# Reordering the prologue of an adaLN block, and one expert's loads on another queue

## The chip, the cores and the metric

The kernel runs on one core of a Trainium2 chip. The metric is the device time of one execution in microseconds (us). Engines: TensorE (PE; its weight loads are PEld), VectorE (DVE), ScalarE (ACT), GpSimd (POOL) and SyncE (SP), which here only issues DMAs. ScalarE can issue DMAs too. Each engine runs its own instructions in order, and waits for the others by semaphores.

## The reference

A transformer block with adaptive LayerNorm on x of 8 batch elements x 512 rows x 256 columns, all in fp32:

```python
mod = (silu(c) @ wmod).reshape(8, 6, 1, 256)
sa, ca, ga, sb, cb, gb = (mod[:, i] for i in range(6))
ga, gb = (sign of each) * maximum(abs of each, 0.25)
h = layernorm(x) * (1 + ca) + sa
x = x + ga * attention(h)          # gated delta rule
h = layernorm(x) * (1 + cb) + sb
x = x + gb * experts(h)            # 2 of 6 experts per batch element
```

The attention projects h to q and k (16 heads of 128), v and z (32 heads), runs a causal convolution of 4 taps and a SiLU over q, k and v, and then a gated delta rule in chunks, whose decays come from h as well:

```python
beta = sigmoid(h @ W_b);  g = -exp(A_log) * softplus(h @ W_a + dt_bias)
g = cumsum(g within a chunk);  decay = exp(g[i] - g[j]) for j <= i
```

The experts take the mean of h over the 512 rows, choose the two best of six, and compute `gelu(h @ W1 + b1) @ W2 + b2` for both, weighted by a softmax of the two.

## The kernel before, in words

The work is cut into 128 pairs: 8 batch elements x 16 key heads, each with its two value heads. A chunk is 128 rows, so a batch element has 4. The steps of a pair (`wk`, `pk`, `ck`, ... with places in the table `PLACE`, L26) are spread over about 13 turns of 1000 places each, so that many pairs are in flight; L1292 sorts all steps of all pairs by turn and place, and they are issued in that order under a manual schedule. The side steps of a batch element are put among them: `after_attention(b)` (L325: second LayerNorm, experts) and `before_attention(b + 1)` (L232: first LayerNorm of the next element, its beta and its decays).

What stands ahead of the manual schedule is arranged by the framework's own scheduler: the constants, the block `pro` (L478 to L524) and `before_attention(0)` (L525). In `pro`, ScalarE's queue loads the modulation's weights `wm` (ten of the twelve column blocks) and `wg6` (the two gates), SyncE's the condition `ct` and small tensors. `mps` (L501) is the modulation for both LayerNorms: 8 blocks x 2 halves of the contraction = 16 matmuls of 8 columns, which the profile shows as 32 records. `gps` (L512) is the gates; four DVE instructions (L518 to L521) make them at least 0.25 in size, and L522 writes them to DRAM (`gates_far`), from where `gates(b)` (L172) spreads them much later.

`before_attention(0)` begins with `norm_transposed` (L178): statistics on DVE, `rs` by a power on POOL (L195), then xn = (x - mean) * rs on DVE (L200, eight pieces, four buffers), transposes on TensorE (`lnT`, L208) and scale and shift on ScalarE (`ha`, L216). Then `ba` (L241: 8 matmuls), `beta` (L249), the softplus as a series (L253 to L284: 18 DVE instructions and one exp on ScalarE), the sums of the decays (`dec`, L292), their exp (`ex`, L297), `G` and `neg` (L301, L303), `G` transposed (`Gt`, L308, L312) and written to DRAM (`gfar`, L316).

For each pair, SyncE loads `wk` (L570, two DMAs of 128 KB) and `gb` (L585: rows of `gfar`, spread to 128 partitions, 512 KB). TensorE projects `prk` and `prq` (L614), ScalarE makes tap 0 (L626), DVE taps 1 to 3 (L630), ScalarE the SiLU (`kqa`, L643). Transposes `kt` and `qt` follow, their squares on ScalarE (`jk` L676, `jq` L712), roots on POOL (`kept`, L682), and the decays of the pair: `dca` (L724) reads `gb` and `G` on ScalarE, exp (L732). A change of function set on ScalarE shows as ACT_TABLE_LOAD.

`wk` lives in the pool `wp` (L538), which takes the memory of the pool `pro` after it has been released, so its first load waits for the last users of `pro`. PSUM has six banks for turns (`bank`, L112).

In the last batch element `after_attention(7)` has nothing beside it. `expert(k)` (L381) and `expert_biases(k)` (L395) each load the chosen index into a register of the issuing engine (L379), and then issue three DMAs for the weights and four for the biases, all on SyncE. `gelu` (L427) needs the biases; its second third holds hidden units of both experts.

Of the kernel before, what the change touches and what calls it, by code (L numbers as in the profile page):

```python
# [15 lines left out]
P = 128  # L16
# [71 lines left out]
def adaln_block(  # L88
# [26 lines left out]
    def bank(name):  # L115
        return banks.tile([P, 512], F32, name=name, tag="b")
# [208 lines left out]
    def after_attention(b):  # L325
# [50 lines left out]
            f["v2"] = tiny("b2", [P, 2, DM])  # L376

        def of_choice(k):
            return nc.sync.value_load(f["ix"][0:1, k : k + 1], min_val=0, max_val=NE - 1)  # L379

        def expert(k):  # L381
            if k == 0:
                experts()
            e = of_choice(k)
            nc.sync.dma_start(
                f["s1"][:, :, k * DFF : (k + 1) * DFF],
                w1[bass.ds(e, 1)].rearrange("e (kt p) f -> p (e kt) f", p=P),
            )
            for at, t, q, n in hidden_parts(k, 0, DFF):
                nc.sync.dma_start(  # L390
                    f["s2"][q : q + n, t, :],
                    w2[bass.ds(e, 1), at : at + n, :].rearrange("e p m -> (e p) m"),
                )

        def expert_biases(k):  # L395
            e = of_choice(k)
            for half in range(2):
                for at, t, q, n in hidden_parts(k, half * FP, FP):
                    at -= half * FP
                    nc.sync.dma_start(  # L400
                        f["v1"][q : q + n, t : t + 1],
                        b1[bass.ds(e, 1), at : at + n, half : half + 1].rearrange("e p t -> p (e t)"),
                    )
            nc.sync.dma_start(f["v2"][:, k, :], b2[bass.ds(e, 1)].to_broadcast([P, DM]))

        def weigh():

# [67 lines left out]
        return steps  # L475


    with tc.tile_pool(name="pro", bufs=1) as pro:  # L478
        ct = pro.tile([P, NKT, NB], F32, name="ct")
        nc.sync.dma_start(ct, cond.rearrange("(kt p) b -> p kt b", p=P))  # L480
        wm = pro.tile([P, NKT, 10, P], F32, name="wm")
        nc.scalar.dma_start(
            wm, wmod[:, : 10 * P].rearrange("(kt p) (i m) -> p kt i m", p=P, m=P)
        )
        wg6 = pro.tile([P, 2, NKT, DM], F32, name="wg6")
        for i, col in enumerate((2 * DM, 5 * DM)):
            nc.scalar.dma_start(
                wg6[:, i], wmod[:, col : col + DM].rearrange("(kt p) m -> p kt m", p=P)
            )
        nc.sync.dma_start(wba, w_ba.rearrange("(kt p) m -> p kt m", p=P))  # L490
        nc.sync.dma_start(dtb, dt_bias.partition_broadcast(P))
        nc.sync.dma_start(alog, a_log.partition_broadcast(P))
        nc.sync.dma_start(cw, conv_w)
        nc.sync.dma_start(nw, norm_w)
        nc.sync.dma_start(gwt, gate_w.rearrange("(kt p) e -> p kt e", p=P))
        nc.scalar.activation(silu_c, ct, AF.Silu)

        mps = bank("mps")
        for i, col in enumerate((0, 1, 2, 3, 6, 7, 8, 9)):
            for kt in range(NKT):  # L500
                mm(  # L501
                    mps[:, i * NB : (i + 1) * NB], wm[:, kt, col, :], silu_c[:, kt, :],
                    start=kt == 0, stop=kt == NKT - 1,
                )
        nc.vector.tensor_copy(modt, mps[:, : 8 * NB].rearrange("p (i b) -> p i b", b=NB))
        for i in (2, 6):
            nc.vector.tensor_scalar_add(modt[:, i : i + 2, :], modt[:, i : i + 2, :], 1.0)

        gps = bank("gps")
        for i in range(2):  # L510
            for kt in range(NKT):
                mm(  # L512
                    gps[:NB, i * DM : (i + 1) * DM], silu_c[:, kt, :], wg6[:, i, kt, :],
                    start=kt == 0, stop=kt == NKT - 1,
                )
        gv, ga = (pro.tile([NB, 2 * DM], F32, name=n) for n in ("gv", "ga"))
        nc.scalar.copy(gv, gps[:NB])
        nc.vector.scalar_tensor_tensor(ga, gv, -1.0, gv, ALU.mult, ALU.max)  # L518
        nc.vector.tensor_scalar_max(ga, ga, 0.25)
# [17 lines left out]
    with ExitStack() as st:  # L537
# [800 lines left out]
```

## Time and profile before

| | us |
|---|---|
| time, median of 3 runs (lowest, highest) | 4062.34 (4062.27, 4062.44) |
| time of the profiled execution | 4061.08 |
| its span, first to last instruction | 4059.4 |
| PE busy, share of the span | 3847.1, 95% |
| DVE busy | 3528.6, 87% |
| ACT busy | 3169.1, 78% |
| POOL busy | 1462.0, 36% |

Lines of the profile: an `L` number is the line of the kernel; `out<-in` are tiles by their names in the program with buffer numbers left out; `xN` counts instructions. A timeline line is start, duration, engine, line, operation, and in brackets the idle time ahead of it with the one who ended it. SPq and ACTq are the queues' own instructions, such as the issue of a DMA. A chain line is start, duration and what it was. A line for a stretch of time gives for PE, PEld, DVE, ACT and POOL busy time (and instructions), then the granted TensorE clock, the DMA engines' busy share, and GB/s.

### The profile page before, as it was taken

Reading aid. Unit: us, or ns where it says so; the run is one execution under the profiler, and the core shown is the slowest. Engines: PE = TensorE matmul, PEld = TensorE weight load, DVE = VectorE, ACT = ScalarE, POOL = GpSimd, SP = SyncE. Lnnn points to the kernel's source line nnn. Section 1 sums busy time; section 2 is a strip of 40 time slices with the busy share of each in tenths; the row PEclk is TensorE's granted clock in tenths of the full one; section 3 lists DMA queues with packets and bytes.
Section 4 is the critical chain, followed back from the end, with each engine's and each line's share of the span. In section 5 each row is a group of like instructions: output and inputs, shape, how many; then the busy total and the mean of one; then the engine's idle time right before and its main releaser. Section 6 shows DMA issues by size and latency. Waiting matters only on the chain.

```text
span 4059.4 us, 79959 instructions
## 1 busy us (share of the span) xinstructions
PE 3847.1 (95%) x24592; PEld 2771.3 (68%) x24592; DVE 3528.6 (87%) x7973; ACT 3169.1 (78%) x9809; POOL 1462.0 (36%) x1320
## 2 busy tenths in 40 slices
PE   5489999999999999999999999999999999999998
PEld 3256776767776677767777667767677667776776
DVE  4689888998989988998889988899888998899864
ACT  5578778878878788778888778888888878877664
POOL 3433333333333333433334333334333333333211
PEclk8799999999999999999999999999999999999999
DMA  4576667667666676666677566566766667666541
GB/s 119 148 182 170 184 177 192 172 173 187 158 180 185 177 179 179 169 173 185 174 177 187 161 188 178 171 184 174 184 169 172 182 179 188 164 176 179 144 115 55
DMA packets 1101589, 689.09 MB, mean 170 GB/s; under 512 B 667368, under 2 KB 964712, under 8 KB 1101168
## 3 DMA queue, kind: packets, MB, share of 16 engines
q1 hardware_dynamic: 1100352, 682.14, 63.7%
q8 instruction: 203, 3.33, 0.3%
q14 instruction: 218, 1.79, 0.1%
q10 hardware_dynamic: 816, 1.84, 0.1%
HBM read 435.68 MB, written 248.00 MB: 168 GB/s over the span
## 4 chain that ended last, share of the span: by engine, by line
PE 66%; DVE 22%; ACT 4%; issue 4%; DMA 2%; POOL 1%; SPq 0%; POOLq 0%; DVEq 0%; ACTq 0%
PE prz L1200 9%; PE prv L614 8%; PE acc L1244 7%; PE in L1153 4%; PE u L1109 4%; PE dst L1131 4%; PE kk L739 4%; PE prq L614 4%; PE pk L1079 3%; PE prk L614 3%; DVE prl L863 3%; PE pq L1084 3%; PE ot L1226 2%; DVE cvk L630 2%; PE vt L1035 2%
## 5 line engine op out<-in xcount | busy, mean ns | idle before, releaser
L1216 POOL TENSOR_TENSOR msq<-msq,mhalf 128x8 f32<-128x8 f32 x128 | 209.4, 1636 | 1228.5 <-DVE msq L1210 1228.5
L630 DVE SCALAR_TENSOR_TENSOR cvv<-prv,cw,cvv 128x511 f32<-128x511 f32 (+2 forms) x768 | 567.6, 739 | 12.3 <-ACT cvv L626 8.7
L762 POOL TENSOR_TENSOR mta<-mta,dca 128x512 f32<-128x512 f32 x256 | 366.6, 1432 | 510.7 <-DVE mta L750 297.2
L614 PE MATMUL prv<-ha,wv 128*128 128x512 f32 x1024 | 486.7, 598 | 4.5 <-DVE vr L1042 4.5
L1200 PE MATMUL prz<-ha,wz 128*128 128x512 f32 x1024 | 485.8, 597 | 1.5 <-ACT tmp L1100 0.7
L1244 PE MATMUL acc<-wo,z 128*128 128x256 f32 x2048 | 484.3, 379 | 0.5 <-DVE z L1232 0.5
L682 POOL TENSOR_TENSOR kept<-kept,half 128x8 f32<-128x8 f32 x128 | 210.1, 1641 | 727.6 <-ACT jq L712 627.7
L1244 PEld LDWEIGHTS acc<-wo,z 128*128 128x128 f32 x2048 | 378.5, 190 | 46.8 <-DVE z L1232 1.1
L769 POOL TENSOR_TENSOR dca<-qkm,dca 128x256 f32<-128x256 f32 x512 | 394.9, 792 | 32.0 <-issue 7.4
L1100 ACT ACTIVATE tmp<-pq,ex 128x128 f32<-128x128 f32 x768 | 243.5, 378 | 152.9 <-PE pq L1084 152.6
L1153 PE MATMUL in<-w,s 128*128 128x128 f32 x2048 | 317.0, 277 | 23.7 <-DVE cvk L630 19.5
L1153 PEld LDWEIGHTS in<-w,s 128*128 128x128 f32 x2048 | 298.4, 191 | 54.2 <-DVE cvk L630 25.8
L724 ACT ACTIVATE dca<-gb,G 128x128 f32<-128x128 f32 x1024 | 332.9, 428 | 2.7 <-DMA sfar<-dca 2.5
L1124 ACT ACTIVATE w<-u,kept 128x128 f32<-128x128 f32 x1024 | 302.0, 363 | 28.6 <-DVE wd L1116 27.8
L1175 ACT ACTIVATE jo<-o 128x128 f32<-128x128 f32 x1024 | 305.6, 304 | 4.1 <-DVE o L1166 0.8
L614 PEld LDWEIGHTS prv<-ha,wv 128*128 128x128 f32 x1024 | 191.8, 191 | 152.1 <-issue 124.7
L630 DVE SCALAR_TENSOR_TENSOR cvk<-prk,cw,cvk 128x511 f32<-128x511 f32 (+2 forms) x384 | 283.8, 739 | 4.3 <-ACT cvk L626 3.9
L630 DVE SCALAR_TENSOR_TENSOR cvq<-prq,cw,cvq 128x511 f32<-128x511 f32 (+2 forms) x384 | 283.4, 738 | 0.8
L1232 DVE SCALAR_TENSOR_TENSOR z<-ot,nw,z 128x512 f32<-128x512 f32 x256 | 190.8, 746 | 103.1 <-PE ot L1226 97.1
L1200 PEld LDWEIGHTS prz<-ha,wz 128*128 128x128 f32 x1024 | 180.3, 190 | 140.0 <-issue 122.9
L739 PE MATMUL kk<-kqa 128*128 128x256 f32 x1024 | 273.2, 393 | 0.0
L1090 DVE SCALAR_TENSOR_TENSOR r<-pk,neg,vr 128x128 f32<-128x128 f32 x768 | 231.6, 343 | 45.9 <-PE pk L1079 45.7
(204 smaller groups left out, 10052.1 us busy)
## 6 DMA issues: line engine op xcount, KB each, us to landing
gb<-gfar SPq DMA_DIRECT2D x128, 512.0 KB
qfar<-kqa SPq DMA_DIRECT2D x128, 512.0 KB
sfar<-dca SPq DMA_DIRECT2D x256, 256.0 KB
s<-sfar SPq DMA_DIRECT2D x256, 256.0 KB
wk<-in_dram SPq DMA_DIRECT2D x256, 128.0 KB
kfar<-kra SPq DMA_DIRECT2D x128, 256.0 KB
wv<-in_dram SPq DMA_DIRECT2D x128, 256.0 KB
kq<-qfar SPq DMA_DIRECT2D x128, 256.0 KB
```

The costliest lines, as they stand in the source:

```text
L614: mm(ps, d[wname][:, kt, j * P : (j + 1) * P], hT[:, kt, :], start=kt == 0, stop=kt == NKT - 1,)
L630: nc.vector.scalar_tensor_tensor(a[:, s:], ps[:, : SEQ - s], cw[:, ch, 3 - s : 4 - s], a[:, s:], ALU.mult, ALU.add)
L724: nc.scalar.activation(dc[:, c, h, :], d["gb"][:, 2 * gr + c, h * P : (h + 1) * P], AF.Relu, bias=rows[b]["G"][:, 2 * gr + c, k : k + 1], ...
L739: mm(ps[:, c2 * 2 * P : (c2 + 1) * 2 * P], d["kqa"][:, c, 0, :], d["kqa"][:, c].rearrange("p k i -> p (k i)"), start=True, stop=True,)
L762: nc.gpsimd.tensor_tensor(mt, mt, d["dc", gr].rearrange("p c h i -> p (c h) i"), ALU.mult)
L769: nc.gpsimd.tensor_tensor(dc, bc_mid(d["qkm", gr][:, c, :], 2), dc, ALU.mult)
L1100: nc.scalar.activation(tmp[:, h, :], d["pq", c][:, h * P : (h + 1) * P], AF.Copy, scale=rows[b]["ex"][:, 0, c, 2 * p + h : 2 * p + h + 1],)
L1124: nc.scalar.activation(w[:, h, :], d["u", c][:, h * P : (h + 1) * P], AF.Copy, scale=d["br2"][:, c, h : h + 1],)
L1153: mm(ps[:, h * P : (h + 1) * P], d["s", c, h], d["w", c][:, h, :], start=True, stop=True,)
L1175: nc.scalar.activation(junk, d["o", c // 2][:, c % 2, h, :], AF.Square, accum_out=d["msq"][:, c, h : h + 1],)
L1200: mm(ps, d["wz"][:, kt, h * P : (h + 1) * P], rows[n // HK]["ha"][:, kt, :], start=kt == 0, stop=kt == NKT - 1,)
L1244: mm(ps[:, k * DM : (k + 1) * DM], d["z", h][:, c * P : (c + 1) * P], d["wo"][:, h, :], start=p == 0 and k == 0 and h == 0, stop=p == HK - ...
```

## The change

`before_attention(0)` is no longer run as one block after `pro`. `wm` is loaded in two DMAs (4 and 6 blocks), and the modulation is computed in two halves: the first LayerNorm's, then the steps of `before_attention(0)` up to the softplus, with beta's sigmoid as the last, then the second LayerNorm's half. The gates' result `ga` gets a tile of its own outside `pro` (`gate_rows`), and its DMA to DRAM is put at the place TURN of the manual schedule. The exp of `alog` is moved up. The rest of element 0's decays (`gs`, `gx`, `gr`, `gt`, `gc`, `gl`) is put into the manual schedule just ahead of the first pair's `gb`, and so behind `wk`, `pk`, `ck`, `pq`, `cq` and `sk` of the first pair. For the last batch element's second expert (k == 1), the index load and all seven DMAs go to ScalarE's queue.

```diff
         def of_choice(k):
-            return nc.sync.value_load(f["ix"][0:1, k : k + 1], min_val=0, max_val=NE - 1)
+
+            queue = nc.scalar if b == NB - 1 and k == 1 else nc.sync
+            return queue, queue.value_load(f["ix"][0:1, k : k + 1], min_val=0, max_val=NE - 1)
...
-            e = of_choice(k)
-            nc.sync.dma_start(
+            queue, e = of_choice(k)
+            queue.dma_start(
                 f["s1"][:, :, k * DFF : (k + 1) * DFF],
...
+    first_steps = before_attention(0)
+    gate_rows = row.tile([P, 2, DM], F32, name="gate_rows", tag="of", bufs=1)
     with tc.tile_pool(name="pro", bufs=1) as pro:
...
-        nc.scalar.dma_start(
-            wm, wmod[:, : 10 * P].rearrange("(kt p) (i m) -> p kt i m", p=P, m=P)
-        )
+        for a, e in ((0, 4), (4, 10)):
+            nc.scalar.dma_start(
+                wm[:, :, a:e, :],
+                wmod[:, a * P : e * P].rearrange("(kt p) (i m) -> p kt i m", p=P, m=P),
+            )
...
-        mps = bank("mps")
-        for i, col in enumerate((0, 1, 2, 3, 6, 7, 8, 9)):
...
+        nc.scalar.activation(alog, alog, AF.Exp)
+        nc.vector.tensor_scalar_mul(alog, alog, -1.0)
+
+        def modulation(half):
+
+            ps = bank(f"mps_{half}")
+            for i in range(4):
+                for kt in range(NKT):
+                    mm(
+                        ps[:, i * NB : (i + 1) * NB], wm[:, kt, 6 * half + i, :], silu_c[:, kt, :],
+                        start=kt == 0, stop=kt == NKT - 1,
+                    )
+            m = modt[:, 4 * half : 4 * half + 4, :]
+            nc.vector.tensor_copy(m, ps[:, : 4 * NB].rearrange("p (i b) -> p i b", b=NB))
+            nc.vector.tensor_scalar_add(m[:, 2:4, :], m[:, 2:4, :], 1.0)
+
+        modulation(0)
+        for name in list(first_steps):
+            if name not in ("bsig", "gs", "gx", "gr", "gt", "gc", "gl"):
+                first_steps.pop(name)()
+        first_steps.pop("bsig")()
+        modulation(1)
...
-        gv, ga = (pro.tile([NB, 2 * DM], F32, name=n) for n in ("gv", "ga"))
+        gv = pro.tile([NB, 2 * DM], F32, name="gv")
+        ga = gate_rows[:NB].rearrange("p a b -> p (a b)")
         nc.scalar.copy(gv, gps[:NB])
...
-        nc.sync.dma_start(gates_far, ga)
-        nc.scalar.activation(alog, alog, AF.Exp)
-        nc.vector.tensor_scalar_mul(alog, alog, -1.0)
-    for step in before_attention(0).values():
-        step()
...
             order += [(at + PLACE[name], fn) for name, fn in side.items()]
+
+        order += [(PLACE["gb"] - 0.5, fn) for fn in first_steps.values()]
+        order.append((TURN, lambda: nc.sync.dma_start(gates_far, ga)))
         order.sort(key=lambda e: e[0])
```

`expert_biases` gets the same replacement of `nc.sync` by `queue` as `expert`.

More of the change, by code (lines that the diff above doesn't have):

```diff
@@ L389, in expert @@
             for at, t, q, n in hidden_parts(k, 0, DFF):
-                nc.sync.dma_start(
+                queue.dma_start(
                     f["s2"][q : q + n, t, :],
@@ L395, in expert_biases @@
         def expert_biases(k):
-            e = of_choice(k)
+            queue, e = of_choice(k)
             for half in range(2):
@@ L399, in expert_biases @@
                     at -= half * FP
-                    nc.sync.dma_start(
+                    queue.dma_start(
                         f["v1"][q : q + n, t : t + 1],
@@ L403, in expert_biases @@
                     )
-            nc.sync.dma_start(f["v2"][:, k, :], b2[bass.ds(e, 1)].to_broadcast([P, DM]))
+            queue.dma_start(f["v2"][:, k, :], b2[bass.ds(e, 1)].to_broadcast([P, DM]))
         def weigh():
@@ L496, in adaln_block @@
         nc.scalar.activation(silu_c, ct, AF.Silu)
-        mps = bank("mps")
-        for i, col in enumerate((0, 1, 2, 3, 6, 7, 8, 9)):
[L500 to L507, printed above, removed]
+        nc.scalar.activation(alog, alog, AF.Exp)
[17 more added lines that the diff above has]
+        modulation(1)
         gps = bank("gps")
```

## The prediction

> **What bounds the kernel now.** I read the page first: busy time, the slices, the chain that ended last.
>
> ```profile
> PE 3847.1 (95%) x24592; PEld 2771.3 (68%) x24592; DVE 3528.6 (87%) x7973; ACT 3169.1 (78%) x9809; POOL 1462.0 (36%) x1320
> ...
> PE   5489999999999999999999999999999999999998
> ```
>
> TensorE is full from the fourth slice (about 300 us) to the end, and it takes its work in a fixed order. So whatever is gained or lost before that, in the run-up, moves the whole stream. The change touches the first 60 us and the last 25 us only; on every engine the rest keeps its order. Next I read the timeline of the first 62 us (start, us, engine, line, operation, tiles).
>
> ```profile
> 16.63 3.63 POOL L555 MEMSET y<- 128x1024 f32 x4
> 18.62 1.72 DVE L200 TENSOR_SCALAR xn_a<-xt,mv_a,rs_a 128x128 f32<-128x128 f32 x1
> 20.69 0.33 DVE L200 TENSOR_SCALAR xn_a<-xt,mv_a,rs_a 128x128 f32<-128x128 f32 x1
> ...
> 27.02 0.90 SPq L570 DMA_DIRECT2D wk<-in_dram  x2
> ...
> 38.60 0.49 ACT L297 ACTIVATE ex<-dec 128x384 f32<-128x384 f32 x1 [7.23 <-PE dec L292]
> ...
> 39.74 3.62 PE L614 MATMUL prk<-ha,wk 128*128 128x512 f32 x4
> ...
> 40.30 0.34 SPq L316 DMA_DIRECT2D gfar<-Gt  x1
> ...
> 41.87 0.37 SPq L585 DMA_DIRECT2D gb<-gfar  x1
> ...
> 48.98 0.63 ACT L643 ACTIVATE kqa<-cvq 128x512 f32<-128x512 f32 x1 [0.50 <-DVE cvq L630]
> ...
> 50.20 1.27 ACT L724 ACTIVATE dca<-gb,G 128x128 f32<-128x128 f32 x4
> ...
> 53.58 1.64 POOL L682 TENSOR_TENSOR kept<-kept,half 128x8 f32<-128x8 f32 x1 [33.32 <-ACT jq L712]
> ```
>
> To be seen: gfar leaves at 40.30, gb is fetched at 41.87, and the first dca, which reads gb, runs at 50.20. Behind dca on ScalarE stand jq, kra, jk, jq, and the last jq releases POOL's kept at 53.58. From there the chain of waits goes kept, scalars, mta, taps of pair 1, kqa of pair 1 and so on: the last jq of the next pairs ends at about 67.4, 81.8 and 95.9, one pair each 14 us, with ScalarE almost without a gap. A delay of the first dca is therefore carried into the whole run-up. How long gb takes is in the DMA rates (last column GB/s):
>
> ```profile
> 43.00:44.00 1.00, 1.00 (x2) 0.34 (x1) 0.00 (x0) 0.56 (x1) 0.00 (x0) 1.00 0.31 89
> 47.00:48.00 1.00, 0.00 (x0) 0.00 (x0) 0.96 (x2) 0.99 (x2) 0.00 (x0) 1.00 0.88 87
> 48.00:49.00 1.00, 0.47 (x2) 0.47 (x3) 0.85 (x2) 0.50 (x2) 0.00 (x0) 0.56 0.82 186
> ```
>
> gb's 512 KB flow at 88 GB/s from 43.0, so they end at 48.5 to 48.9; with 0.3 us to the semaphore (gfar's bytes end at 41.6, gb is issued at 41.87) gb lands 7.1 us after its issue, near 49.0. The dca at 50.20 has only 1.2 us to spare. Last, the chain at the end:
>
> ```profile
> 4035.18 0.35 SPq L379
> ...
> 4043.49 2.02 DMA b<-in_dram
> 4045.51 0.02 issue
> ...
> 4045.61 0.48 ACT hid L430
> 4046.09 0.04 issue
> 4046.14 2.52 PE f L439 x10
> ```
>
> From 4035.18 to 4043.49 SyncE issues one expert DMA after another; the bias of expert 1 ends the wait of the GELU.
>
> **The change part by part: the head.** All times on the clock of the trace before.
>
> *Modulation split.* It takes 8 of 16 matmuls (3.5 of 7.0 us) from before the LayerNorm. wm's bytes stay the same, and ct, which releases silu_c at 11.40, comes behind xt on SyncE's queue as before. So the first half ends at 15.05 instead of 18.48. In the new order DVE's copy of it stands ahead of the first xn, which is ready at 15.2. POOL's memsets (L555) run until 20.26. Row: the xn of 18.62 took 1.72 us where others take 0.33; it began in the third y memset, was passed by the fourth, and ended 0.08 after it. Rule: the Trainium skill (SBUF – State Buffer, "Who interferes with whom") says that DVE's two-port modes and GpSimd share a port pair that is locked for one whole instruction, first come first served. By the rule xn would enter when the running memset ends, at about 15.7; by the row it waits for the last one, to 20.3. I take the row, as it shows a boundary (19.36) not used; the rule's sum stands with the rivals. Then: four xn to 21.1 (0.28 each), transposes 0.5 behind them, ha0 at 21.7 (before 23.04), ha1 at 23.5 (25.35): a gain of 1.8.
>
> *What is put in front of ba on PE.* The second modulation half (16 records x 0.22 = 3.5) and half of gps (4 x 0.45 = 1.8) now precede the 14 remaining ba records (3.3): 23.3+3.5+1.8+3.3 = 31.9 for g, before 29.78. Loss against before: 2.1.
>
> *Decay series and gates.* beta now stands behind g on ScalarE, with the table switch after it: sps at 34.2 (before 31.40, +2.8). The four gate rows (0.60+0.35+0.34+0.67 = 2.0) are now woven into DVE's series after the reciprocal: the last ends at 38.3.
>
> *First weights.* In the built order wk of pair 0 waits for exactly that last gate row (it reads gv, whose memory wk's pool takes over). Before it waited for gates_far, to 27.02, with 10 us to spare; now it is issued at 38.45. Its bytes before ended near 28.65, so landing is 1.9 after issue: 40.4. prk starts at 40.4, not 39.74 (+0.65). So the decays beside the projections do not bring the projections forward; the g series (7 us) is hidden, but the load has taken its place.
>
> *Projections, then decays.* prk 3.4, cvk's taps end 47.1. prq: TensorE's records went from 0.86 to 0.43 us at 44.8, 5 us after prk began; shifted or later, prq ends 46.4 (46.0 to 47.2; before 45.81). cvq to 47.15, silu table 1.28, kqa of k to 49.06. Now come the added switches: exp table 1.30, ex 0.49, G at 50.9 (before 39.12: +11.8), Gt and its copy 1.2, gfar at 52.1 (40.30), gb at 53.65, landing 60.75. kqa of q is late too, behind DVE's second and third tap (which now stand after G and Gt) and a third table: 53.5+1.3 = 54.8, to 55.4 (before 49.6), but that is covered by gb, 5 us later. dca therefore starts at 60.75 instead of 50.20: **+10.55**. wk of pair 1 follows gb on SyncE, lands at 61.6; prk and prq end near 68, when ScalarE wants them: at most 0.3, I take 0.15. gates_far moves past 8 issues to where SyncE waited 3.3 for dca: hidden; without that cover 0.4.
>
> The price of a table switch: each row of ACT_TABLE_LOAD is 1.28 and the next ACTIVATE starts 1.30 after it. The Trainium skill (ScalarE: Activation LUTs, "What ACT_TABLE_LOAD costs") gives about 2.66 us with a drain of 1.38. One added switch is on the path to gb, so the page would make the sum 1.4 larger; no row here shows the drain (cvq ends 46.54, table 46.56), so I take the row.
>
> **The tail.** Expert 1's seven DMAs (and two loads of its index) leave SyncE's queue. A row of ScalarE's queue is near SyncE's (wm 0.48 against 0.34 to 0.40). ScalarE starts after the choice's exp, at 4035.4: 2.4 us for the weights, 2.8 for the biases, which is SyncE's cadence, plus about 0.7 because its third bias now shares a semaphore with SyncE's first and waits for its landing: 4041.4. Queued behind are the GELU table and the GELUs only: table to 4042.7 (before 4044.0). Expert 1's w1 lands 2.0 earlier, so PE's 12 hidden records (0.43 each) run from 4038.56 without a gap, to 4043.75 or, if PE's pace doubles sooner than at 4045.1, 4043.1. GELU 2 ends 4044.2, and the ten records of 4046.14 start at about 4044.2. Gain 1.3 (slow pace until 4045.8) to 2.7; I take **2.0**. If ScalarE's issues took twice their time, the table would stand at 4046 and nothing would be gained.
>
> **Sum.** 10.55 + 0.15 - 2.0 = +8.7. The profiled execution took 4061.08 (span 4059.4), so 4069.8; the median of the runs, 4062.34, lies 1.26 higher: **4071.0**. 0.2% is 8.1 us, about what a measurement of this kernel can tell from no change, so the forecast lies just past it.
>
> **The rivals.**
>
> *Not slower: DVE gets in between the memsets.* Place: the first xn, 15.2. If the lock is given per memset and DVE runs several instructions on end, ha0 comes at 17.3, ba ends at 27.4, and all behind it (gates, wk, prk, gb) is 4.5 earlier: 4066.5, within 0.2%. It decides as soon as it gives back 0.6 us. For it: the rule. Against it: the row of 1.72.
>
> *Faster, as its words say: the decays are hidden.* Even with wk there in time, prk would start at 33.7, 6.7 earlier, and gb still lands at 54, 3.8 later than dca wanted it: the total would be +1.9, 4064. So a gain above 8 us would need gb off the path, and nothing in the order does that.
>
> *The run-up absorbs it.* If a DMA or PE rather than ScalarE set the pace of pairs 1 to 8, part of the 10.7 would be lost in waits that exist already: at half, 4066. Against: waits on DMA in that stretch are some 8 us for prk in 200 us, and all their DMAs are issued behind the same chain.
>
> *Worse.* If gb and wk of pair 1 delay prk by more (slow pace throughout 3.4 us), the drain of the page applies, or the ScalarE queue gains nothing: +11 to +13, 4074.
>
> **How the numbers follow.** Forecast 0.65, its own range 4069 to 4073 (PE's pace 0.7, gb's landing 0.3, tail 0.7), six tenths of it past 4070.5; DVE between the memsets 0.15; absorbed or hidden 0.08; worse 0.12. Slower: 0.65x0.6 + 0.12 and a little of the rest, 0.52; within 0.2%: 0.43; faster 0.05, for what I have not seen. Range 4065 to 4074: it takes in the first two rivals and the near end of the last.
>
> **What would show it.** xn ending at 20.3 with POOL; g near 31.9; wk issued at 38.4 behind the last gate row; two more table loads around ex; gfar at 52, dca at 60 to 61 waiting for DMA; kept at 64 (before 53.58), and the next pairs 14 us apart. In the tail ScalarE's issues done by 4041.5 plus the shift, and the GELU no longer waiting for a bias. Wrong it would be if dca starts before 57, or if the shift of kept is not found again at 300 us.

## The result: 7.6 us slower, where 8.7 were forecast

The changed kernel takes 4069.64 us (median of 18 runs, 4067.46 to 4072.79), the kernel before, on the same chip, 4062.03 (18 runs, 4060.20 to 4064.84): ratio 1.0018, interval 1.0011 to 1.0026, or +7.6 us. The profiled execution took 4068.49 against 4061.08, its span 4066.8 against 4059.4: +7.4. So the changed kernel lies near the edge of what a measurement tells from no change, and by its interval on the slower side of no change. The sum of the forecast was +8.7 (profiled execution 4069.8), the likeliest time 4071.0. About 1.3 of the 1.4 between 4071.0 and 4069.64 lie in the sum; the step from the profiled execution to the median, taken as 1.26, came out as 1.15.

The page of the changed kernel first (busy time, the slices of TensorE, and of the costliest groups the one of dca):

```profile
PE 3844.3 (95%) x24592; PEld 2768.4 (68%) x24592; DVE 3533.1 (87%) x7974; ACT 3170.8 (78%) x9811; POOL 1462.1 (36%) x1320
...
PE   5479999999999999999999999999999999999998
...
L737 ACT ACTIVATE dca<-gb,G 128x128 f32<-128x128 f32 x1024 | 332.9, 428 | 7.6 <-DMA gb<-gfar 5.4
```

TensorE is as full as before from the fourth slice on. The last line is the finding in small: of the 7.6 us that ScalarE stands idle ahead of all 1024 dca, 5.4 are one wait for gb. It is here, in the timeline of the first 70 us (start, us, engine, line, operation):

```profile
6.32 0.90 ACTq L493 DMA_DIRECT2D wg<-in_dram  x2
6.63 0.75 DVE L187 BATCH_NORM_STATS2 st_a<-xt 128x6 f32<-128x256 f32 x2 [5.53 <-DMA xt<-in_dram]
...
12.54 5.87 DVE L200 TENSOR_SCALAR xn_a<-xt,mv_a,rs_a 128x128 f32<-128x128 f32 x1
...
14.70 3.63 POOL L568 MEMSET y<- 128x1024 f32 x4
...
35.48 0.89 SPq L583 DMA_DIRECT2D wk<-in_dram  x2
37.79 3.75 PE L627 MATMUL prk<-ha,wk 128*128 128x512 f32 x4 [6.42 <-DMA wk<-in_dram]
...
48.24 0.49 ACT L297 ACTIVATE ex<-dec 128x384 f32<-128x384 f32 x1
...
49.80 0.34 SPq L316 DMA_DIRECT2D gfar<-Gt  x1
...
51.36 0.37 SPq L598 DMA_DIRECT2D gb<-gfar  x1
...
59.14 1.28 ACT L737 ACTIVATE dca<-gb,G 128x128 f32<-128x128 f32 x4 [5.41 <-DMA gb<-gfar]
...
62.52 1.64 POOL L695 TENSOR_TENSOR kept<-kept,half 128x8 f32<-128x8 f32 x1 [44.18 <-ACT jq L725]
```

ex comes at 48.24 where it was at 38.60, gfar at 49.80 (40.30), gb at 51.36 (41.87), dca at 59.14 (50.20) and kept at 62.52 (53.58). The last two are both 8.94 late. At the end of the program, where the expert numbers are found, the shift is 8.83 (4043.72 against 4034.89), and the last VectorE instruction is 7.41 late: so the tail gave back 1.42. Its chain that ended last:

```profile
4046.01 3.20 DMA w<-in_dram
4049.23 0.33 ACTq L402
...
4050.45 1.96 DMA b<-in_dram
4052.41 0.03 ACTq L432
...
4052.68 0.48 ACT hid L432
```

In this chain the GELUs stand behind a bias again, now one that ScalarE issued. The timeline shows one thing more in front of them, the load of the GELU table:

```profile
4051.38 1.28 ACT L432 ACT_TABLE_LOAD   x1 [7.15 <-DMA b<-in_dram]
```

The bias has landed at 4052.41, the table load ends at 4052.66 and the first GELU starts at 4052.68: the table load ends last, by 0.25. It stands in ScalarE's order behind ScalarE's own four bias issues, and the first of these, of 4049.23, had waited 3.20 us for the landing of SyncE's second w2 piece, because both use one completion counter (the semaphore that tells of a transfer's landing; an issue that takes it over waits until the transfer that had it before has landed).

### The profile page after: what moved, and what is told of

The parts are those of the page before. It is cut to its first block, busy times and chain, and to the rows that moved or that the text cites. A ratio compares the mean times of both kernels' runs of the same rounds, so it can differ in the third digit from the quotient of the medians.

```text
span 4066.8 us, 79963 instructions
## 1 busy us (share of the span) xinstructions
PE 3844.3 (95%) x24592; PEld 2768.4 (68%) x24592; DVE 3533.1 (87%) x7974; ACT 3170.8 (78%) x9811; POOL 1462.1 (36%) x1320
## 4 chain that ended last, share of the span: by engine, by line
PE 67%; DVE 22%; ACT 3%; issue 3%; DMA 2%; POOL 1%; SPq 0%; POOLq 0%; ACTq 0%; DVEq 0%
PE prz L1213 9%; PE prv L627 8%; PE acc L1257 7%; PE in L1166 4%; PE u L1122 4%; PE dst L1144 4%; PE prq L627 4%; PE kk L752 4%; PE pk L1092 3%; PE prk L627 3%; PE pq L1097 3%; DVE prl L876 3%; PE ot L1239 2%; PE vt L1048 2%; DVE cvk L643 2%
## 5 line engine op out<-in xcount | busy, mean ns | idle before, releaser
L1166 PEld LDWEIGHTS in<-w,s 128*128 128x128 f32 x2048 | 298.4, 191 | 52.1 <-DVE cvk L643 23.4
```

The lines of the kernel that those rows point to most:

```text
L1166: mm(ps[:, h * P : (h + 1) * P], d["s", c, h], d["w", c][:, h, :], start=True, stop=True,)
```

## Experiments

The theory on trial: the six decay steps stand behind the first projections, so gb is asked for late, and the delay passes whole into the run-up. Rivals: the wait of wk for the gate rows, the wait of xn for GpSimd's fills, a run-up that absorbs, a tail that gains nothing. Since medians scatter by 2 us here, I read each kernel's time together with three instants of its profile: the first kept, the last chunk pair's kept, and the stretch from the expert numbers (the indices of the two chosen experts) to the last VectorE instruction. The two columns of kept are differences to before, which is given in full; the last column is the stretch itself, in us.

| kernel | median us | ratio to before, interval | first kept | last pair's kept | numbers to last VectorE |
|---|---|---|---|---|---|
| before | 4061.7 to 4062.5 | | 53.58 | 3765.44 | 20.44 |
| changed | 4069.64 | 1.0018 (1.0011, 1.0026) | +8.9 | +8.8 | 19.02 |
| tail | 4060.63 | 0.9996 (0.9988, 1.0005) | -0.7 | +1.6 | 19.29 |
| head | 4072.87 | 1.0025 (1.0015, 1.0034) | +9.0 | +10.6 | 20.42 |
| inplace | 4064.02 | 1.0003 (0.9994, 1.0011) | +1.8 | +4.3 | 19.23 |
| gatesout | 4068.13 | 1.0014 (1.0008, 1.0021) | +6.0 | +8.9 | 19.53 |
| wmsplit | 4060.01 | 0.9992 (0.9984, 1.0001) | -3.7 | -1.2 | 24.08 |
| memearly | 4065.35 | 1.0010 (1.0002, 1.0019) | +2.8 | +6.3 | 19.45 |
| tail2 | 4073.83 | 1.0030 (1.0019, 1.0042) | +9.8 | +10.8 | 22.44 |
| best4 | 4065.16 | 1.0006 (0.9998, 1.0015) | -6.2 | +1.7 | 23.00 |
| wglate | 4062.66 | 1.0000 (0.9991, 1.0009) | -1.8 | -1.7 | 20.45 |
| best5 | 4056.68 | 0.9986 (0.9980, 0.9993) | -5.4 | -2.4 | 19.24 |
| best6 | 4055.79 | 0.9982 (0.9975, 0.9989) | -5.9 | -3.2 | 18.38 |

### The two halves of the change alone

**tail**: the kernel before with the second edit alone.

```diff
-            return nc.sync.value_load(f["ix"][0:1, k : k + 1], min_val=0, max_val=NE - 1)
+            queue = nc.scalar if b == NB - 1 and k == 1 else nc.sync
+            return queue, queue.value_load(f["ix"][0:1, k : k + 1], min_val=0, max_val=NE - 1)
...
```

> The kernel before with the second half of the change alone: the very last choice's weights and biases are issued by ScalarE, the head of the program is as before. Theory (the tail gained about 1.4 us, because the GELUs no longer wait for a bias; what is left of the wait is the third b1 piece, held on ScalarE by a completion counter that it shares with a weight load of the other queue): the first 64 us as before (first kept at 53.6), the last VectorE instruction 1.4 us sooner after the expert numbers are found, time about 4060.6. Rival 1 (the tail gained nothing, and the whole difference of the changed kernel, +7.6, is its head's): 4062.0. Rival 2 (the full 2.0 of the forecast is there): 4060.0.

Measured: 4060.63, 1.7 below the kernel before, with an interval that includes no change. The profile decides: from the numbers to the last VectorE instruction 19.29 us, 1.15 less than before. In the head, which the edit doesn't touch, the first kept comes 0.7 earlier: so far two runs of one head can differ.

**head**: the changed kernel, last expert on SyncE.

```diff
-            queue = nc.scalar if b == NB - 1 and k == 1 else nc.sync
+            queue = nc.sync
```

> The changed kernel with its last expert back on SyncE, so the head of the change alone. Theory (first chunk pair starts 8.9 us late because its decay broadcast gb is issued 9.5 us later, and this is carried whole to the end): first kept at 62.5 (53.6 before), expert numbers found 8.9 us later than before, time 4062.0 + 8.9 = 4070.9, with the tail's waits for a bias as in the kernel before. Rival 1 (the later chunk pairs absorb part of the delay): first kept at 62.5 too, but under 4067. Rival 2 (the tail of the changed kernel gained nothing): 4069.6, as the changed kernel.

Measured: first kept 62.58, the last pair +10.6, the tail 20.42 as before, median +10.5. Rival 1 falls: nothing is absorbed. Rival 2 falls by the profile, as the tail without the edit takes 1.4 longer. That the median is 2 above the 4070.9 is more than the theory says, and its interval (1.0015 to 1.0034, +6.1 to +13.8) holds both. The extra 1.6 between the first kept and the last arose in one step ahead of pair 11 (counted from 0), where TensorE's granted clock is 0.5 for 10.2 us (from 259.8) in head and for 3.4 us (from 249.5) in before; such steps are told of below.

### The decays, the gates and the fills

**inplace**: the decay steps back where they were, ahead of the projections; the rest as changed.

```diff
+    for fn in first_steps.values():
+        fn()
...
-        order += [(PLACE["gb"] - 0.5, fn) for fn in first_steps.values()]
```

> The changed kernel with one thing put back: the six decay steps of batch element 0 run after the gate rows and before the first projections, as in the kernel before; split modulation, interleaved order and the ScalarE queue stay. Theory (what costs is that gb is asked for behind the first projections, their convolution taps and two table loads): G leaves VectorE after the gate rows, about 35.5, gfar is written at about 36.6, gb is issued at about 38 and lands before 46, so the first chunk's products follow the keys and queries again, 10.5 after prk as in the kernel before: prk 37.8, first kept at about 52 (53.6 before, 62.5 in the changed kernel), and with the tail about 4058.8 (4057 to 4061), faster than before. Rival 1 (the load of wk behind the gate rows is what delays the first chunk): prk and with it all the rest stay where they are in the changed kernel, kept 60 or later, 4067 or more. Rival 2 (the delay of xn behind GpSimd's fills is what counts): the same, kept 60 or later.

```profile
35.37 2.23 DVE L277 SCALAR_TENSOR_TENSOR spe<-spe,spz 128x128 f32<-128x128 f32 x7
35.51 0.89 SPq L585 DMA_DIRECT2D wk<-in_dram  x2
...
40.38 0.49 ACT L297 ACTIVATE ex<-dec 128x384 f32<-128x384 f32 x1 [8.06 <-PE dec L292]
...
43.81 0.37 SPq L600 DMA_DIRECT2D gb<-gfar  x1
...
50.58 0.63 ACT L658 ACTIVATE kqa<-cvq 128x512 f32<-128x512 f32 x1 [0.32 <-DVE cvq L645]
...
55.37 1.64 POOL L697 TENSOR_TENSOR kept<-kept,half 128x8 f32<-128x8 f32 x1 [37.00 <-ACT jq L727]
```

gb is issued at 43.81 instead of 51.36, the wait for it is gone (dca follows kqa of q at 51.98), and the first kept comes 7.15 us earlier than in the changed kernel. Both rivals, which said 60 or later, fall: the place of the decays, put back alone, is worth 7.15 of the 8.94. The expected 52 was not reached, since I had forgotten the series: its seven L277 start at 35.37, behind the gate rows woven into it, so ex comes at 40.38 (38.60 before) and kept 1.8 after before's, where I had expected 1.6 ahead of it.

**gatesout**: gv in a buffer outside `pro`, so wk waits for TensorE's gate projection alone.

```diff
-        gv = pro.tile([NB, 2 * DM], F32, name="gv")
+        gv = row.tile([P, NF, 2 * P], F32, name="gv_rows", tag="hid", bufs=1)[:NB].rearrange("p t m -> p (t m)")[:, : 2 * DM]
```

> The changed kernel with the tile gv kept outside the pool pro, in a buffer that nothing else uses then, so that wk_0 waits only for the last reading of the prologue's tiles by TensorE (gate projection, ends about 31.4) and not for the last gate row on VectorE (35.40). Theory (the decays queue behind the first projections, so an earlier wk moves the whole chain prk, taps, ex, G, gfar, gb with it): wk issued at about 31.5, prk at 33.8 (37.8 in the changed kernel), gfar at about 46, first kept at about 58.5, time about 4065.7: half of the loss remains. Rival 1 (the wait of wk is the whole cause): first kept back to about 54, time at or below 4061. Rival 2 (VectorE's gate rows hold the first taps, so that an earlier wk gains nothing): kept 62, 4069.

```profile
31.69 0.89 SPq L583 DMA_DIRECT2D wk<-in_dram  x2
...
34.05 3.44 PE L627 MATMUL prk<-ha,wk 128*128 128x512 f32 x4 [2.43 <-DMA wk<-in_dram]
...
41.53 0.93 DVE L277 SCALAR_TENSOR_TENSOR spe<-spe,spz 128x128 f32<-128x128 f32 x3
...
46.70 0.34 SPq L316 DMA_DIRECT2D gfar<-Gt  x1
...
59.59 1.64 POOL L695 TENSOR_TENSOR kept<-kept,half 128x8 f32<-128x8 f32 x1 [41.00 <-ACT jq L725]
```

wk is issued 3.79 earlier and prk starts 3.74 earlier, but gfar and kept gain 3.10 and 2.93 only: the series, till then hidden under the wait for wk, now comes out between the taps of cvk (the L277 up to 42.46). The wait of wk is thus a part of the loss, not the whole: rival 1 falls, rival 2 too. It is a smaller part than expected (2.9 at the first kept and not 4; 4068.13 and not 4065.7).

**memearly**: GpSimd's ten fills ahead of everything it does for the norm.

```diff
+    w1b = ctx.enter_context(tc.tile_pool(name="w1b", bufs=1))
...
+    for t in (xl, yl, m5, x5, w5, m6, x6, w6, *ysb):
+        nc.gpsimd.memset(t, 0.0)
...
     silu_c = res.tile([P, NKT, NB], F32, name="silu_c")
...
-        for t in (xl, yl, m5, x5, w5, m6, x6, w6, *ysb):
-            nc.gpsimd.memset(t, 0.0)
```

> The changed kernel with GpSimd's ten fills (xl, yl, m, x, w, y; 8.6 us) moved ahead of the first norm's rs_a, to the start of the program; everything else as in the changed kernel. Theory (xn stands in VectorE from 12.5 to 18.4 because GpSimd fills memory, and the split modulation is worth nothing until they are out of the way): rs_a starts about 10.5 and not 8.8, xn's first row takes 0.2 us and not 5.9 and starts at about 12.6, everything up to gb is about 5.5 earlier: g at 24, wk at 30, first kept at 57, time about 4064. Rival 1 (the fills at the start hold bn_stats or rs_a as long as they held xn): first kept 61 to 63, 4068 to 4070. Rival 2 (the gate weights or wm's second half land too late for an earlier start): PE waits for a DMA before gps or the second half, first kept 59 or later, 4066 or more.

```profile
8.56 1.92 DVE L202 TENSOR_SCALAR rs_a<-mv_a 128x4 f32<-128x4 f32 x1
10.56 1.02 POOL L205 TENSOR_TENSOR rs_a<-rs_a,mhalf 128x4 f32<-128x4 f32 x1
...
12.99 0.31 DVE L210 TENSOR_SCALAR xn_a<-xt,mv_a,rs_a 128x128 f32<-128x128 f32 x1
```

The first xn takes 0.31 us and not 5.87, and the first kept comes 6.19 earlier than in the changed kernel (expected 5.5). The wait did not vanish: VectorE's rs_a now stands 1.92 us in the fills, where 0.17 is its own time; but the modulation is not ready before 12.6 anyway, so it costs nothing. Rivals 1 and 2 fall. (What inplace, memearly and gatesout win adds up to 16.3, more than the 8.94, since the fills and the gate rows stood in the way before the change too.)

### Why x and cond landed earlier

**wmsplit**: the kernel before, with wm loaded in two parts.

```diff
-        nc.scalar.dma_start(
-            wm, wmod[:, : 10 * P].rearrange("(kt p) (i m) -> p kt i m", p=P, m=P)
-        )
+        for a, e in ((0, 4), (4, 10)):
+            nc.scalar.dma_start(
+                wm[:, :, a:e, :],
+                wmod[:, a * P : e * P].rearrange("(kt p) (i m) -> p kt i m", p=P, m=P),
+            )
```

> The kernel before with one thing changed: the load of wm goes out as two transfers (512 and 768 columns' worth), as in the changed kernel. This measures by itself the term that the forecast lacked. Theory (the rows of x and of cond land earlier because of the two transfers, and that is why everything up to the gate rows stood about 2 us earlier in the changed kernel than forecast): first bn_stats at about 6.6 (8.6 before), table load of the Silu at about 7.3 (9.9), xn done about 1.9 earlier, first kept at about 51.7 (53.6 before), time about 4060.1. Rival 1 (the earlier arrival belongs to the other order of issues in the changed kernel, not to the split): bn_stats at 8.6, kept 53.6, 4062. Rival 2 (the second part of wm lands late and holds the modulation's products): kept 53.6 or later, 4062 or more.

bn_stats at 6.46 (8.55 before), first kept 49.90: -3.7, not -1.9, since cond gains more than x: TensorE is through the modulation and begins the gate projection at 15.54 instead of 18.37, 2.8 earlier, and the transposes follow it. The split alone does it; rivals 1 and 2 fall. (Its tail of 24.08 was held by a bias of SyncE's that landed 3.50 us after its issue, in before 1.51, and by 3.4 us at a granted clock of 0.5. Its edit reaches the tail only by shifting the completion counters, and no issue there waited for one; why the bias took longer is open.) But it left two causes: the split also holds the first wg load to 6.13, from 1.32 before, as that load now shares a completion counter with wm's first part, still under way.

**wglate**: the kernel before, wm whole, the wg loads behind the Silu.

```diff
-        for i, col in enumerate((2 * DM, 5 * DM)):
-            nc.scalar.dma_start(
...
         nc.scalar.activation(silu_c, ct, AF.Silu)
+        for i, col in enumerate((2 * DM, 5 * DM)):
+            nc.scalar.dma_start(
```

> The kernel before with wm whole, as it was, but with the two loads of the gate weights wg (512 KB together) issued by ScalarE after the Silu of the condition and not right after wm. Two causes stand for the 2 us by which the rows of x land earlier once wm is split: (a) the first wg load, which in the kernel before starts at 1.3 us, is held until 6.3 there, so its bytes no longer share the engines with those of x and cond; (b) the smaller transfers of wm themselves let the other queue in. Under (a) bn_stats starts at about 6.6 to 7 here too (8.55 before), the Silu's table load at about 7.5 (9.9 before), first kept 2 to 4 us earlier than 53.6, unless the gate weights themselves come late for TensorE. Under (b) bn_stats stays at about 8.5 and kept at 53.6.

The timeline of before, then that of this kernel, and then that of wmsplit:

```profile
8.55 0.75 DVE L187 BATCH_NORM_STATS2 st_a<-xt 128x6 f32<-128x256 f32 x2 [7.45 <-DMA xt<-in_dram]
```

```profile
8.31 0.75 DVE L187 BATCH_NORM_STATS2 st_a<-xt 128x6 f32<-128x256 f32 x2 [7.21 <-DMA xt<-in_dram]
8.69 0.90 ACTq L494 DMA_DIRECT2D wg<-in_dram  x2
```

```profile
6.13 0.90 ACTq L489 DMA_DIRECT2D wg<-in_dram  x2
6.46 0.75 DVE L187 BATCH_NORM_STATS2 st_a<-xt 128x6 f32<-128x256 f32 x2 [5.36 <-DMA xt<-in_dram]
```

With wg out of the way x lands 0.24 earlier and no more. So (a) falls, and it is the form of wm's own transfer that lets SyncE's queue in. How, the traces show, which count packets by queue. From 3.5 to 5.0 us (queue 10 is ScalarE's, queue 1 SyncE's; packets, MB, share of the 16 DMA engines), in before and then in wmsplit:

```profile
q10 hardware_dynamic: 100, 0.51, 83.8%
q1 hardware_dynamic: 104, 0.11, 19.9%
```

```profile
q10 hardware_dynamic: 191, 0.39, 68.1%
q1 hardware_dynamic: 194, 0.20, 37.2%
```

Both queues get through about as many packets, and a packet here is one row: 5 KB for wm whole (1280 values of 4 bytes), 2 KB for its first part, 1 KB for x. With the shorter rows of wm the turn comes round nearly twice as often, and x moves 0.20 MB instead of 0.11 in the same time. That agrees with the Trainium skill (DMA: Bandwidth & Descriptors, "Queues, rings and completion order"), which says that each engine takes turns between the queues packet by packet. The Silu is helped in another way too: in wglate it comes at 8.68 (11.18 before) though x hardly moved, as ScalarE loads its table at 1.32 and not behind its second wg issue, which waits for cond's counter and ended at 9.86. The modulation so starts 2.5 earlier (8.95), and the first kept is 1.8 earlier, where (b) had expected no change. By time wglate settles nothing (4062.66).

### Building a better kernel

**tail2**: on ScalarE the biases first, the weights after.

```diff
+            if b == NB - 1 and k == 0:
+                expert_biases(1)
...
-            "eb1": lambda: expert_biases(1)
+            "eb1": lambda: None if b == NB - 1 else expert_biases(1)
```

> The changed kernel, with the tail's issues in another order: ScalarE issues the second choice's biases first and its weights after, so that no bias issue of ScalarE shares a completion counter with a weight load of SyncE that is under way. Theory (1.2 us or more of the tail's gain was lost because the third b1 piece waited 3.2 us for w2_0b's landing on a shared counter, and the table load and GELUs queue behind it): ScalarE's last issue ends about 4 us after the expert numbers are found plus 1 (7.6 after in the changed kernel), the first GELU is held by its product and by the other queue's biases, about 7 after the numbers (9.0 in the changed kernel), last VectorE instruction 17.5 after them (19.1), time about 4068. Rival 1 (the GELUs were held by the products or by the first choice's biases anyway): no gain, 4069.6. Rival 2 (the second choice's weights, now issued later, hold the second layer): last VectorE instruction 20 or more after the numbers, 4071.

```profile
4051.07 0.41 ACTq L389 DMA_DIRECT2D w<-in_dram  x1
...
4054.89 3.75 PE L426 MATMUL f<-hb,w 128*128 128x256 f32 x8 [3.40 <-DMA w<-in_dram]
```

22.44 from the numbers to the last VectorE instruction instead of 19.02: I had looked only at the second layer. The second third of the hidden units reads both choices' w1, which is issued 4.2 later behind the biases (5.41 after the numbers instead of 1.26), and TensorE waits 3.40 for it. Rival 2's 20 or more came, though at the first layer.

**best4**: memearly, gatesout, inplace and tail2 together, with the gate rows moved to the start of the second pair.

```diff
+        def gate_values():
+            nc.vector.scalar_tensor_tensor(ga, gv, -1.0, gv, ALU.mult, ALU.max)
+            nc.vector.tensor_scalar_max(ga, ga, 0.25)
+            nc.vector.tensor_scalar(gv, gv, 0.0, 2.0, ALU.is_ge, ALU.mult)
+            nc.vector.scalar_tensor_tensor(ga, gv, -1.0, ga, ALU.add, ALU.mult)
+            nc.sync.dma_start(gates_far, ga)
+        order.append((TURN, gate_values))
```

> What the experiments point to, together: split modulation and tail with the biases first, GpSimd's fills at the start, gv outside the pool so that wk waits for the gate projection alone, the six decay steps ahead of the first projections, and the four gate-row instructions moved from the front of the decays' series to the start of the second chunk pair. Theory (each of the four waits that the runs have shown is worth what it was measured at): g at about 24, the series ends about 31, ex about 33, prk about 34 (39.7 before), first kept at about 48 (53.6 before, 62.5 in the changed kernel), tail 3 shorter than before, time about 4054 (4052 to 4057). Rival (something else holds the first chunk pair, such as wk's landing or the gate weights): first kept 52 or later, 4058 or more.

```profile
54.18 1.52 DVE L642 SCALAR_TENSOR_TENSOR cvq<-prq,cw,cvq 128x511 f32<-128x511 f32 x2
...
55.62 0.67 DVE L1307 SCALAR_TENSOR_TENSOR gate_rows<-gv_rows 8x512 f32<-8x512 f32 x1
...
58.14 0.73 DVE L642 SCALAR_TENSOR_TENSOR cvq<-prq,cw,cvq 128x509 f32<-128x509 f32 x1
```

First kept 47.33, as expected, but 4065.16. The gate rows stand in front of the last tap of cvq, and the second kept is only 3.4 ahead of before, the third 1.7, the fifth 0.6. And the tail of tail2 costs 2.6 against before.

**best5** and **best6**: the gate rows behind the last tap of the first pair (an order value just past `cq3`), where VectorE had nothing to do; the tail of the change in best5; in best6 both choices' biases on SyncE, and on ScalarE the second choice's weights alone. Against best4:

```diff
-            nc.sync.dma_start(gates_far, ga)
...
-        order.append((TURN, gate_values))
+        order.append((PLACE["cq3"] + 0.5, gate_values))
+        order.append((TURN, lambda: nc.sync.dma_start(gates_far, ga)))
...
-            queue, e = of_choice(k)
+            queue, e = nc.sync, nc.sync.value_load(f["ix"][0:1, k : k + 1], min_val=0, max_val=NE - 1)
```

(The last two lines, in `expert_biases`, are best6's alone.)

> As the combined kernel, with two things different: the four gate-row instructions of VectorE run after the last convolution tap of the first chunk pair, where VectorE stood idle from 42.7 to 49.0, and not between the taps of the second pair; and the tail is the changed kernel's own (weights first on ScalarE). Theory (the combined kernel won 6.2 us at the first kept and lost it again over the next four pairs because 2.6 us of gate rows stood between the taps of the second pair, and it lost 3.5 in the tail because the second choice's w1 landed late): first kept at 47.3 (53.6 before), second at 61.4, and 6 earlier than before at the fifth pair too; from the numbers of the experts to the last VectorE instruction 19.1 (20.5 before); time about 4055 (4053 to 4057). Rival (a gain at the first pair is not carried, whatever the gate rows do, since the following pairs wait for their own transfers): the fifth kept within 2 of before, 4060 or more.

> As the kernel beside it, with the biases of both choices on SyncE and the second choice's weights alone on ScalarE. Theory (the Gelu's table and the first GELU wait in ScalarE's order behind its bias issues, which wait for w2_0b's landing on a shared counter): ScalarE's table load comes 4 us earlier, the first GELU is held by its product, the second and third by the second choice's biases; last VectorE instruction 18.4 after the expert numbers (19.1 with ScalarE's biases, 20.5 before), time 0.7 below the kernel beside it. Rival 1 (the second choice's biases, last in SyncE's order, hold the second GELU as much as before the change): 20 to 20.5 after the numbers, 1 above the kernel beside it. Rival 2: no difference.

```profile
33.07 0.49 ACT L307 ACTIVATE ex<-dec 128x384 f32<-128x384 f32 x1 [6.21 <-PE dec L302]
...
36.32 0.37 SPq L595 DMA_DIRECT2D gb<-gfar  x1
...
43.09 0.67 DVE L1305 SCALAR_TENSOR_TENSOR gate_rows<-gv_rows 8x512 f32<-8x512 f32 x1
...
47.67 1.64 POOL L692 TENSOR_TENSOR kept<-kept,half 128x8 f32<-128x8 f32 x1 [36.10 <-ACT jq L722]
```

Both beat the kernel before: 4056.68 (ratio 0.9986, interval 0.9980 to 0.9993) and 4055.79 (0.9982, 0.9975 to 0.9989; -6.8 us). Between the two the medians differ by 0.9, which the scatter doesn't settle; from the numbers to the end the profiles show 19.24 and 18.38, the 0.7 expected and a little more. The table load came 1.4 earlier than in best5, not the 4 expected: it now waits for the landing of a bias of the first choice.

The gain is not carried as the loss was. In best5 5.4 at the first pair are 3.4 at the third and 2.1 at the fifth, between the "within 2 at the fifth" of the rival and the 6 of the theory; in best6, which has the same head, 5.9 become 5.45 and 3.9. One wait is to be seen, at the last dca of the second pair. In before, in best5 and in best6:

```profile
68.02 1.28 ACT L724 ACTIVATE dca<-gb,G 128x128 f32<-128x128 f32 x4 [0.49 <-DMA sfar<-dca]
```

```profile
64.60 1.28 ACT L734 ACTIVATE dca<-gb,G 128x128 f32<-128x128 f32 x4 [2.50 <-DMA sfar<-dca]
```

```profile
62.81 1.28 ACT L734 ACTIVATE dca<-gb,G 128x128 f32<-128x128 f32 x4 [1.19 <-DMA sfar<-dca]
```

It is 3.4 and 5.2 earlier than in before, and in front of it ScalarE waits 2.50 and 1.19 for a transfer out of the same buffer, where it waited 0.49. So 0.7 of the gain end there in both. The other 1.3 that best5 loses are not of its order of work, which best6 shares: there SyncE's issue of m6far, just ahead of that transfer, took 1.71 us (0.61 in best6 and in before). I have not tried another buffer for dca, and where the rest of the gain goes is not shown.

## Why the prediction was right

*The main step held: gb, behind ex, behind the projections, sets the first dca.* Forecast +10.55 at dca, measured +8.94, carried to the first kept (+8.94) and to the end (+8.83, and +9.0 and +10.6 in head). The sign at 300 us came too: the shift of kept is 10.9 there (10.7 in head). inplace takes 7.15 of it away by undoing that one move. Against the forecast's clock the steps came evenly early: the modulation's first half done at 12.4 (forecast 15.05), g at 29.60 (31.9), the wk issue at 35.48 (38.45), prk at 37.79 (40.4), ex from 48.24, gfar at 49.80 (52.1), gb at 51.36 (53.65).

*The term that was mis-sized is the arrival of x and cond.* The step said that wm's bytes stay the same and that ct comes behind xt as before, so nothing moves. x landed 1.9 us earlier (bn_stats 6.63 against 8.55) and the Silu's table load began 2.6 earlier (7.25 against 9.89); wmsplit shows that the split does this alone, wglate that it is not the held wg load, and the packets how. What counts in the changed kernel is x: with it GpSimd's rs_a comes 1.9 earlier (8.76 against 10.68), with rs_a the fills behind it, which end at 18.33 instead of 20.26, and with the fills xn. cond's part is lost, as the half modulation is done at 12.4 and xn waits for the fills. Of the -2.3 at gb 1.9 are this; 0.4 came in small steps behind it.

*gb's landing was sized too short.* From its issue to dca 7.78, not 7.1: +0.7. The 7.1 was too short for before already: there gb's completion counter is full at 49.56, 7.69 after the issue, and the dca at 50.20 had 0.6 to spare, not 1.2. The sum had divided gb's bytes by 88 GB/s up to the end, but from 47.9 on gb shares the engines with the rows of the next wk. Together -1.6, the difference between 10.55 and 8.94. That the total came so near is partly luck: -2.3 for the head's clock stands against +0.7 here and +0.6 in the tail.

*xn and the fills: the row held.* The first xn ended at 18.41, 0.08 after GpSimd's last fill, as in the row of before. The Trainium skill's rule (SBUF – State Buffer, "Who interferes with whom"), as the forecast applied it, by which xn would have entered when the fill running at 12.54 ended, at about 12.9, would have ended it some 5.2 us earlier; eight fills began after it and went ahead of it. In memearly, rs_a on VectorE waited in the same way to the end of the fills.

*The table switches.* Two more of 1.28 us, with no drain to be seen: the ACTIVATE behind one starts 1.29 after it began (46.95 and 48.24). So the row was the better choice there too.

*wk behind the last gate row* held: it is issued 0.08 after that row ends (35.40), and gatesout shows what the wait is worth: 2.9.

*Pair 1.* The 0.15 taken for its late wk was not there: the second kept comes 14.03 after the first, in before 14.02.

*The tail* gave 1.4, not 2.0. The shared counter was seen and taken as 0.7 for ScalarE's issues, to 4041.4 on the clock of before; they ended at 4051.30, which less 8.83 is 4042.5. The wait for the landing of w2 lasted longer than thought, and best6, without it, gets 0.86 more than best5. The sign that I named, a GELU that no longer waits for a bias, came by 0.25 us only: the first GELU waits for its table, and the table load waits in ScalarE's order for the bias issues. best6, with no bias issue on ScalarE, loads the table 6.3 after the expert numbers and not 7.7.

*The rivals.* DVE between the fills: falls by xn. Absorbed: falls by head. Decays hidden: falls, gb was waited for 5.41 us. Worse: none of its three causes came (the second pair was not held up more, no drain, and ScalarE's queue did gain 1.4), but the median of head (+10.5) shows how near it would have been without the tail's gain.

## What to carry over

What is moved behind a stage takes its transfers along: ex here moved for the sake of a hidden 7 us series, and the chain that counted was Gt, gfar, gb and an 8 us landing behind it. Before moving work, ask which transfer it releases and how long that takes, and look for an idle stretch of the engine that nothing waits for (VectorE's after the last tap took the gate rows for nothing, while the same four instructions in the next pair cost 2.9 us). A delay ahead of the full pipeline was carried whole here; of a gain a part ended at waits that had been almost there before (from the first kept to the last, 5.4 became 2.4 in best5, and 5.9 became 3.2 in best6).

## What the runs showed of the chip

**The scatter of 2 us has a grain.** Pair by pair the kernels keep their distance to 0.1 us for hundreds of us, and then it changes in a step of up to 1.6. Between pairs 100 and 101 the changed kernel's kept goes from +10.1 to +8.8, and nine of the other eleven kernels make the same step at the same pair; memearly and best6 do not. Before, memearly and best6 are also the three whose traces have 3.4 us at a granted clock of 0.5 at that place, so the disturbance is in the profile of before, and in theirs. Before's stretches of time, and those of tail (busy time by engine, then granted TensorE clock, DMA share, GB/s):

```profile
2940.00:2960.00 20.00, 20.00 (x125) 14.99 (x124) 17.30 (x42) 18.30 (x52) 10.05 (x10) 1.00 0.72 202
2960.00:2970.00 10.00, 8.10 (x54) 5.37 (x54) 9.47 (x19) 5.17 (x18) 0.00 (x0) 0.83 0.72 200
```

```profile
2941.70:2961.70 20.00, 20.00 (x125) 14.98 (x124) 17.29 (x43) 18.30 (x52) 10.02 (x10) 1.00 0.88 223
2961.70:2970.00 8.30, 6.40 (x54) 4.33 (x53) 8.10 (x16) 4.43 (x16) 0.00 (x0) 1.00 0.71 190
```

The same stretch of work takes 10.0 us in before and 8.3 in tail, at a granted clock of 0.83 and 1.00: after a gap of 1.9 us on TensorE, four matmuls of the experts take 1.91 us instead of 1.03. Tail had a gap of 1.90 at the same place and kept its clock. The Trainium skill (TensorE: Matmul & The Clock Gate, "Part 1: The HAM clock gate") makes the clock depend on how busy TensorE was lately. On what it hangs here, the 13 traces show together. In each, every change of the granted clock lies on a grid of 3.41 us. Between 280 and 3990 us TensorE has 94 gaps of 1.85 to 1.96 us: of the 44 that lie whole inside one step of the grid, 35 are followed by a step at half clock; of the 50 that the border of two steps cuts, one is, and it misses a step by less than 0.06 us. So the same gap costs a spell or not by where it falls on the grid, which a shift of 1 us decides. Tail's gap lies inside a step as well and is one of the nine that kept the clock; why is open.

Such spells make the later steps of the shift: up to 11.7 in the changed kernel's own (at 558.9), and back to 8.8 in before's (at 1024.3 and 2963.1). One in tail ahead of pair 11 has prq in 3.78 us where before takes 1.98. The rise from 8.9 to 10.9 lies in the first 300 us, where the clock changes often (13 times to half in before), and I have not taken it apart. For a change of this size the first pairs of the profile tell more than the medians.

**Two queues that share a completion counter wait for each other.** Which transfers share one lies in how the program is built. A new transfer near the front shifts who shares with whom. In this kernel that held ScalarE's wg load from 1.32 to 6.32, and in the tail a bias issue for 3.2 us, with a table load and GELUs behind it.
